# Rows of the first head pair placed by selection matmuls, and the first four pairs processed by halves of their queries

## The chip, the cores and the metric

The kernel runs on one core of one Trainium2 chip. The metric is the device time of one execution in microseconds. Five engines take part, each with its own instruction queue: PE (matmul; PEld is its weight load), DVE (VectorE), ACT (ScalarE), POOL (GpSimd) and SP (SyncE, which here only issues DMAs).

## The reference

Two layers over x of shape (4, 1024, 256): attention with 16 heads of 16 elements, and a mixture of 8 experts (top 2, capacity 1.25), each followed by a residual sum and a layer norm.

```
q, k, v = x @ wq.T, x @ wk.T, x @ wv.T                # per head, 16 elements
q_mag, k_mag = softplus(q), softplus(k)
q_embed = [q_mag * cos(freqs), q_mag * sin(freqs)]     # 32 elements per head
k_embed = [k_mag * cos(freqs + bias), k_mag * sin(freqs + bias)]
out = softmax(q_embed @ k_embed.T / 4) @ v             # all 1024 keys, no mask
x = layernorm(x + out @ wo.T)
gates = softmax(x @ router_w + router_b); top 2, positions by cumsum, capacity 640
y = sum of gate * (gelu(x @ w1 + b1) @ w2 + b2) over the chosen experts
x = layernorm(x + y)
```

## The kernel before

One program in three parts: a head that loads and prepares, a loop of attention steps, and the experts. The change touches the head and the attention loop; the experts stay as they are.

**Tiling of attention.** A batch has 1024 tokens and 16 heads. Heads go in two groups of eight (index f), each group in four pairs; a pair of one batch is a *unit* u, 32 units in all (`B * NU`). Of a unit, `qk_u` holds four tiles of 128 rows by 1024 columns: for each of the two heads the queries and the keys, as float32r values split in an upper part and a remainder, so that one product over 128 rows gives a score at full precision (for q the rows are cos/sin of the upper part twice, then of the remainder twice; for k the upper part, the remainder, and both again).

**Embedding.** `embedding(b, f, w, h)` makes q or k of all eight heads of a group for one half h of the tokens: a product (L367), softplus by ACT as Abs, Exp, Ln (L384 to L386), then sums, the product with the cos/sin table (L396) and the split in parts (L401 to L405). With `fast` the elementwise work is on DVE and ACT, otherwise on POOL. Its rows come out ordered by element and then head (d, m). The parts are stored in DRAM by four DMAs (L413), and `load_qk(u)` (L419) loads those of one pair, ordered as `qk_u` needs them: 8 DMAs for q (L432) and 4 for k (L436). DRAM is thus what puts rows in another order. In the head, unit 0's rows are stored and loaded by halves of the tokens, k through SP's queue, q through POOL's.

**A step.** Steps run over n = 0 to 255; step n handles unit n // 8 and a block c of 128 keys. It makes `key_scores` (L715: keys by queries, all 1024 queries of both heads, four products of 512 columns), subtracts the row maximum by a product of two rows with ones (`exponentials`, L730), lets ACT take exp (L737, two of 128x1024), and weights the values of the *step before* with them (`weighted_values`, L751). The maximum must be known before a unit's first step: `score_half(u, k, j)` (L688, queries by keys, 512 keys) with a DVE maximum each (L692), 32 of them per unit, then `max_parts` (three small DVE instructions, L698 to L700) and `max_rows` (four transposes on PE, L706, and a copy by ACT, L708). Unit 0's 32 scores stand in the head; from step 1 on each step carries four scores for the unit after (step 0 carries eight more). The results of a unit are copied by ACT (L760) and sent to DRAM and to another tile by six DMAs (`collect`, L779, L782).

**What sets the order.** All of this is under `manual_schedule`: each engine takes its instructions in the order in which the program text emits them. Pieces of other work (embeddings of the next group or batch, transposes, projections, the router) hang in a table `todo`, put there by `at` and `staged` at fixed places (batch, pair, block), and are emitted at the end of that step. Generators (`yield`) cut a piece in parts that are emitted at different places.

**Buffers.** PSUM: three banks `bank` (scores, embeddings, transposes), two double banks `st` (key scores; in the head `rotate` hands them out to others too), one `av`. SBUF pools: `big` (three: weights in duplicate, table 0, then `qk`), `p2` tag `parts`, `p4` tag `pt` (exponentials).

Lines of the profile that matter here: L367 embedding product, L413 store of parts, L432/L436 loads of `qk`, L688/L692 score and maximum, L698 to L708 the maxima's way to a row, L715/L730/L737/L751 a step, L238 store of a table.

## Time and profile before

| what | us |
|---|---|
| median of 3 runs (lowest, highest) | 1468.1 (1467.44, 1471.71) |
| the profiled execution, its own time | 1469.84 |
| its span, first to last instruction | 1468.0 |
| PE busy in the span | 1372.4 (93%) |
| DVE busy | 917.8 (63%) |
| ACT busy | 728.6 (50%) |
| POOL busy | 410.2 (28%) |
| start of the first exponential (step 0) | 64.06 |
| start of the exponentials of step 8 and step 32 | 102.23 and 188.76 |

A matmul's end is modelled, so a busy PE is not PE at its peak: what a piece of work costs is read better from how far apart two like steps start. In the rows of instructions the columns are start, length, engine, line, operation, output<-input, count, and in brackets the idle time before and what ended it.

### The profile page before, as it was taken

The page shows a single profiled execution, that of the slowest core. Times are in us where ns is not written, and L with a number is a line of the kernel's source. Part 1 is how long each engine was busy: PE and PEld are TensorE (multiplying, and loading weights), DVE is VectorE, ACT ScalarE, POOL GpSimd, SP SyncE. Part 2 cuts the span into 40 slices and gives each one's busy share as a digit, 9 for nine tenths or more (in the row PEclk, how much of TensorE's full clock was granted, in tenths as well). Part 3 has the DMA queues.
Part 4 walks back from the last instruction along what each step waited for, and adds up shares of the span by engine and source line. Part 5 has one row for each costly group of instructions (what it writes and reads, how often), then busy time and mean ns, then how long its engine had stood idle before and what let it go on. Part 6 is the DMA issues. An engine that isn't in the chain of part 4 may idle for free. (4 is left out here: it accounts for less than half of the span.)

```text
span 1468.0 us, 24361 instructions
## 1 busy us (share of the span) xinstructions
PE 1372.4 (93%) x9314; PEld 860.1 (59%) x9314; DVE 917.8 (63%) x1990; ACT 728.6 (50%) x944; POOL 410.2 (28%) x436
## 2 busy tenths in 40 slices
PE   5899999999999999999999999999994599999996
PEld 3455556555655565656556555555543377777775
DVE  6767766667877766787766677787715243333334
ACT  5365666565556656555664754655462222222221
POOL 5640043340002646000064520000402224434432
PEclk8799999999999999999999999999996699999998
DMA  7856367374344646453474542243210454333211
GB/s 234 262 161 186 99 189 201 89 226 119 108 120 137 190 128 212 122 153 88 116 216 134 151 135 63 71 105 84 76 58 7 131 181 154 107 115 130 72 40 43
DMA packets 107315, 191.23 MB, mean 130 GB/s; under 512 B 19633, under 2 KB 56178, under 8 KB 107072
## 3 DMA queue, kind: packets, MB, share of 16 engines
q1 hardware_dynamic: 96192, 167.80, 39.6%
q0 software_dynamic: 9888, 20.01, 4.4%
q10 hardware_dynamic: 1120, 1.87, 0.4%
q8 instruction: 73, 1.20, 0.4%
q14 instruction: 42, 0.34, 0.1%
HBM read 119.32 MB, written 73.63 MB: 131 GB/s over the span
## 5 line engine op out<-in xcount | busy, mean ns | idle before, releaser
L692 DVE TENSOR_REDUCE nm<-s 128x1 f32<-128x512 f32 x1024 | 644.6, 683 | 231.7 <-PE s L688 217.3
L737 ACT ACTIVATE pt<-st 128x1024 f32<-128x1024 f32 x512 | 496.2, 1021 | 392.7 <-PE st L730 375.8
L688 PE MATMUL s<-qk 128*128 128x512 f32 x1024 | 390.7, 440 | 23.7 <-DVE nm L692 12.1
L715 PE MATMUL st<-qk 128*128 128x512 f32 x1024 | 308.9, 401 | 4.4 <-ACT pt L737 3.4
L751 PE MATMUL av<-pt,va 128*32 128x256 f32 x4096 | 275.6, 386 | 0.5 <-ACT pt L737 0.5
L688 PEld LDWEIGHTS s<-qk 128*128 128x128 f32 x1024 | 179.9, 191 | 136.6 <-DVE nm L692 58.2
L715 PEld LDWEIGHTS st<-qk 128*128 128x128 f32 x1024 | 182.8, 189 | 68.1 <-ACT pt L737 33.2
L751 PEld LDWEIGHTS av<-pt,va 128*32 128x32 f32 x4096 | 107.2, 109 | 108.2 <-issue 63.0
L652 POOL DMA_INDIRECT slots_in<-held,scatter_idx x64 | 62.6, 977 | 306.0 <-DVE scatter_idx L650 225.1
L390 POOL TENSOR_TENSOR soft_q<-y_q,soft_q 128x512 f32<-128x512 f32 x14 | 17.9, 1279 | 448.0 <-ACT soft_q L386 448.0
L1234 PE MATMUL op<-w,h 128*128 128x256 f32 x640 | 140.6, 379 | 0.0
L1215 PE MATMUL hp<-slots_t,w 128*128 128x320 f32 x512 | 139.8, 434 | 0.0
L1234 PEld LDWEIGHTS op<-w,h 128*128 128x128 f32 x640 | 121.1, 190 | 17.0
L730 PE MATMUL st<-mt,ones_r 2*128 2x512 f32 x1024 | 130.1, 498 | 0.7 <-ACT mt L708 0.7
L1215 PEld LDWEIGHTS hp<-slots_t,w 128*128 128x128 f32 x512 | 97.7, 191 | 39.9 <-ACT slots_t L1068 0.3
L730 PEld LDWEIGHTS st<-mt,ones_r 2*128 2x128 f32 x1024 | 49.2, 182 | 90.0 <-issue 88.6
L1222 ACT ACTIVATE h<-hp,b_sb 128x640 f32<-128x640 f32 x64 | 50.8, 793 | 85.3 <-PE hp L1215 73.0
L1249 DVE TENSOR_TENSOR o<-op,b_sb 128x256 f32<-128x256 f32 x35 | 14.8, 424 | 103.7 <-PE op L1234 99.8
L1250 ACT ACTIVATE o<-o,w 128x256 f32<-128x256 f32 x35 | 17.8, 507 | 109.1 <-DVE o L1249 100.3
L1252 POOL DMA_INDIRECT y_rank<-o,rows x35 | 35.6, 1016 | 109.3 <-ACT o L1250 61.5
L1176 POOL DMA_INDIRECT out_dram<-row,rows x40 | 41.3, 1033 | 44.8 <-DMA out_dram<-row,rows 14.3
L463 DVE TENSOR_TENSOR held<-po,held 128x512 f32<-128x512 f32 x32 | 22.1, 690 | 41.8 <-PE po L455 41.8
(210 smaller groups left out, 1038.3 us busy)
## 6 DMA issues: line engine op xcount, KB each, us to landing
qk<-embed_q SPq DMA_DIRECT2D x248, 128.0 KB
qk<-embed_k SPq DMA_DIRECT2D x124, 256.0 KB
embed_k<-parts_k SPq DMA_DIRECT2D x64, 256.0 KB
w<-in_w_dram SPq DMA_DIRECT2D x16, 1024.0 KB
embed_q<-parts_q SPq DMA_DIRECT2D x56, 256.0 KB
y_rank<-zero SPq DMA_DIRECT2D x8, 1024.0 KB
tab_k<-table SPq DMA_DIRECT2D x14, 512.0 KB
tab_q<-table SPq DMA_DIRECT2D x12, 512.0 KB
```

Of the source, the lines that this page charges most:

```text
L652: nc.gpsimd.indirect_dma_start(out=scatter_views[2 * t + k], out_offset=bass.IndirectOffsetOnAxis(ap=scatter_idx[:, k, t : t + 1], axis=0) ...
L688: nc.tensor.matmul(ps, qk[:, 2 * h, lo : lo + P], qk[:, 2 * h + 1, j * HS : (j + 1) * HS], start=True, stop=True,)
L692: nc.vector.tensor_reduce(nms[u][:, j, i, s : s + 1], ps, AX.X, ALU.max, negate=True)
L715: nc.tensor.matmul(ps[:, f, :], qk[:, 2 * h + 1, c * P : (c + 1) * P], qk[:, 2 * h, f * HS : (f + 1) * HS], start=True, stop=False,)
L730: nc.tensor.matmul(tiles[h][:, f, :], ones_r[rows, :], mts[u][rows, :], start=False, stop=True,)
L737: nc.scalar.activation(pt, tiles[h], AF.Exp)
L751: nc.tensor.matmul(av[32 * s : 32 * (s + 1), cols], va[f][:, c, 2 * p + h, :], pt[h][:, s // 2, cols], start=(c == 0 and n == 0), stop=(c ...
L1176: nc.gpsimd.indirect_dma_start(out=out_views[t], out_offset=bass.IndirectOffsetOnAxis(ap=to[:, 0, t : t + 1], axis=0), in_=row[:, t, :], i ...
L1215: nc.tensor.matmul(ps[:, i, 0:half], w1_sb[:, k, c * P : (c + 1) * P], s_t[:, k, i * half : (i + 1) * half], start=(k == 0), stop=(k == KC ...
L1222: nc.scalar.activation(h_t[:, c, :].rearrange("p (i n) -> p i n", i=2), ps[:, :, 0:half], AF.Gelu, bias=b1_sb[:, e, c : c + 1],)
L1234: nc.tensor.matmul(ps, h_t[:, c, t * P : (t + 1) * P], w2_sb[:, c, :], start=(c == 0), stop=(c == HC - 1),)
L1252: nc.gpsimd.indirect_dma_start(out=y_views[e * ST + t], out_offset=bass.IndirectOffsetOnAxis(ap=to[:, 1, t : t + 1], axis=0), in_=o_sb, in ...
```

## The change

1. **Selection matrices.** POOL builds `picks`, float32r matrices of zeros and ones (two memsets, four selects, two copies), in the head, after its loads of angles.
2. **Unit 0's rows by matmul.** `move_first(w, cols, parts)` multiplies the four parts of an embedding by these matrices: for each of the two heads four products of 512 columns accumulate in one PSUM bank and give the tile in the order that `qk_0` needs; ACT copies it. There are four calls (k and q, two halves of the tokens): 32 products and 8 copies. No load from DRAM for unit 0 remains. The stores of the parts remain (the other pairs load them), now all on SP.
3. **Second half of q on POOL.** `embedding(0, 0, "q", 1)` is no longer `fast`.
4. **Half units.** The first four pairs (batch 0, group 0) are split in two by their queries: 36 entries in `units`, a half unit has 4 steps, and each step handles two blocks of keys for 512 queries. The number of steps stays 256, with the same products in each. A half unit has its own 16 scores, `max_parts`, `max_rows`, copy of results and `collect`.
5. **A plan of scores.** A list `ahead[n]` replaces the fixed four per step: the scores of all units from 1 on are spread so that each is done two steps before its unit starts, and no unit's before the pair ahead of it is about to start. It gives 6 in step 0, 5 in steps 1 to 18, and 4 from step 19 on. Ahead of step 0 stand the 16 scores of half unit 0 only, in place of 32.
6. **Other pieces of the head.** q of group 1 (batch 0) moves from the head into the steps, beside k (starting in steps 2, 5, 8, 11). The second key table is written in pieces: its first half before `max_parts(0)`, its second in steps 1 and 3. The stores of the tables and the load of the second pair come behind the last part of q.

```diff
+        picks = p1.tile([P, 2, 2, 13, HD], F32R, tag="os", name="picks")
+        for h in range(2):
+            pick = p2.tile([P, 2, 13, HD], F32, tag="y", name=f"pick_{h}")
+            nc.gpsimd.memset(pick, 0.0)
+            for w, (first, apart) in enumerate(((5, 2), (3, 4))):
+                blocks = pick[:, w, first : first + apart + 1 : apart, :]
+                nc.gpsimd.affine_select(
+                    out=blocks, in_=blocks, compare_op=ALU.not_equal, fill=1.0, base=-h,
+                    pattern=[[0, 2], [-FH, HD]], channel_multiplier=1,
+                )
+            nc.gpsimd.tensor_copy(picks[:, h], pick)
...
             for i, c in enumerate((nb4, sb4)):
                 nc.scalar.activation(a[:, i, :], cs[:, 1 - i, cols], AF.Copy, scale=c[:, 1:2])
                 nc.scalar.activation(kt[:, i, :], cs[:, i, cols], AF.Copy, scale=cb4[:, 1:2])
-            for i in range(2):
                 nc.gpsimd.tensor_tensor(kt[:, i, :], kt[:, i, :], a[:, i, :], ALU.add)
+                if i == 0:
+                    yield
             store_table(2, h, kt)
...
+        def move_first(w, cols, parts):
+            if 0 not in qks:
+                qks[0] = big.tile([P, 4, S], F32R, tag="big", name="qk_0")
+            k = w == "k"
+            pss = [bank(f"rows_{w}_{h}_{cols.start}", True) for h in range(2)]
+            for p in range(2):
+                for c in range(2):
+                    at = c + (2 if k else 4) * p
+                    first = (3 if k else 5) - at
+                    for h in range(2):
+                        nc.tensor.matmul(
+                            pss[h],
+                            picks[:, h, int(k), first : first + 8, :].rearrange("p b d -> p (b d)"),
+                            parts[p][:, c, :],
+                            start=(p == 0 and c == 0),
+                            stop=(p == 1 and c == 1),
+                        )
+                yield
+            for h in range(2):
+                nc.scalar.copy(qks[0][:, 2 * h + k, cols], pss[h])
+                yield
...
+        for i in range(B * NU):
+            for h in range(2) if i < NU // NF else (None,):
+                starts.append(starts[-1] + lasting[-1] if units else 0)
+                units.append((i, *divmod(i // (NU // NF), NF), i % (NU // NF), h))
+                lasting.append(NT if h is None else NT // 2)
...
+            for x in range(2):
+                h, q, k = (t, x, c) if half is None else (x, half, 2 * c + t)
                 nc.tensor.matmul(
-                    ps[:, f, :],
-                    qk[:, 2 * h + 1, c * P : (c + 1) * P],
-                    qk[:, 2 * h, f * HS : (f + 1) * HS],
+                    ps[:, x, :],
+                    qk[:, 2 * h + 1, k * P : (k + 1) * P],
+                    qk[:, 2 * h, q * HS : (q + 1) * HS],
...
-                if b == 0 and n > 1:
-                    staged(0, ((0, 2), (0, 4))[n - 2], 2, embedding, 0, 1, w, h)
+                if b == 0:
+                    staged(0, ((0, 2), (0, 5), (1, 0), (1, 3))[n], 2, embedding, 0, 1, w, h)
...
+            n_items = max([-((given - i) // (d - n + 1)) for d, i in due if d >= n], default=0)
+            most = max(i for first, i in may if first <= n)
+            ahead[n] = items[given : min(given + n_items, most)]
...
             k0, q0, k1, q1 = first("k", 0), first("q", 0), first("k", 1), first("q", 1)
...
-            load_qk(0, halves[0], "k")
-            for work in (k1, q0, q0):
+            mk0, mq0 = moving("k", 0), moving("q", 0)
+            for work in (mk0, mq0, mk0, mq0):
                 run(work)
-            load_qk(0, halves[0], "q", nc.gpsimd)
             key_table(1)
-            for work in (k1, q1, q1, k1, k1):
+            for work in (k1, q1, mk0, mq0, k0, q0):
                 run(work)
-            load_qk(0, halves[1], "k")
-            for work in (q1, q1):
+            run(k1)
+            mk1 = moving("k", 1)
+            for work in (mk0, mq0):
                 run(work)
-            load_qk(0, halves[1], "q", nc.gpsimd)
             for h in range(2):
                 values(0, 0, h, rotate=True)
-            load_qk(1)
+            for i in range(4):
+                score_half(0, 2 * i, 0)
+            for work in (mk1, mk1, mk1, mk1, k1, q1):
+                run(work)
+            mq1 = moving("q", 1)
+            for i in range(4):
+                score_half(0, 2 * i + 1, 0)
+            for h in range(2):
+                values(0, 1, h, rotate=True)
+            for i in range(4):
+                score_half(0, 2 * i, 1)
+            for i in range(4):
+                score_half(0, 2 * i + 1, 1)
+            for _ in second_key_table(0):
+                pass
+            max_parts(0)
+            max_rows(0, rotate=True)
+            for work in (mq1, mq1, mq1, mq1, q1):
+                run(work)
             for h in range(2):
                 store_table(0, h, cs[:, :, halves[h]])
                 store_table(1, h, kt0[:, :, halves[h]])
+            once("k", 1)
+            once("q", 1)
+            load_qk(1)
             late_constants()
...
+        pieces = second_key_table(1)
+        for c in (1, 3):
+            at(0, 0, c, run, pieces)
```

The lines of the changed kernel that the text names: L452 the selection products, L786 key scores.

## The prediction

> **What bounds the kernel now.** I read the 40 slices first, then busy time by stretches of 3.4 us in the head, then the timeline of ACT, which gives one pair of exponentials per step, then what PE waits for.
>
> ```profile
> PE   5899999999999999999999999999994599999996
> PEclk8799999999999999999999999999996699999998
> ```
>
> From the third slice on PE is full, so what is moved there costs its PE time, and what can be won lies in the first two slices (36.7 us each). There it looks like this (columns: stretch, its length, then busy us and instructions of PE, PEld, DVE, ACT, POOL, then the granted clock, DMA share, GB/s):
>
> ```profile
> 21.40:24.80 3.40, 2.03 (x19) 1.84 (x17) 3.40 (x7) 3.27 (x6) 1.87 (x4) 1.00 0.80 295
> 24.80:28.20 3.40, 0.00 (x0) 0.00 (x0) 3.33 (x6) 1.41 (x3) 1.68 (x4) 1.00 0.70 237
> 28.20:31.60 3.40, 0.01 (x1) 0.04 (x1) 3.40 (x9) 3.20 (x6) 3.40 (x7) 0.50 0.86 263
> 55.50:58.90 3.40, 2.00 (x4) 0.74 (x4) 3.40 (x7) 0.43 (x1) 2.82 (x3) 1.00 0.21 55
> 65.80:69.20 3.40, 3.40 (x7) 1.85 (x7) 3.40 (x7) 0.20 (x1) 0.00 (x0) 0.50 0.89 219
> 69.20:72.60 3.40, 3.40 (x11) 1.97 (x10) 2.43 (x5) 0.00 (x0) 0.00 (x0) 0.50 1.01 245
> ```
>
> PE has nothing from 23.4 to 31.6 (rows on their way to DRAM and back) and then runs scores at the pace of DVE's maxima, one per 0.60 us. The clock is 0.50 from 28.2 to 38.4 and from 58.9 to 72.6. PE's waits in the head are these:
>
> ```profile
> PE s L688 <- DVE parts_q L405: 8.2, 1, 8.2
> PE mp L706 <- DVE m L700: 3.1, 1, 3.1
> PE s L688 <- DMA qk<-embed_q: 2.2, 1, 2.2
> ```
>
> The steps, from ACT's timeline (start, us):
>
> ```profile
> 64.06 1.94 ACT L737 ACTIVATE pt<-st 128x1024 f32<-128x1024 f32 x2 [1.28 <-PE st L730]
> 73.87 1.94 ACT L737 ACTIVATE pt<-st 128x1024 f32<-128x1024 f32 x2 [7.88 <-PE av L751]
> 78.37 1.94 ACT L737 ACTIVATE pt<-st 128x1024 f32<-128x1024 f32 x2 [2.56 <-PE av L751]
> 102.23 1.94 ACT L737 ACTIVATE pt<-st 128x1024 f32<-128x1024 f32 x2 [1.45 <-PE st L730]
> 123.23 1.94 ACT L737 ACTIVATE pt<-st 128x1024 f32<-128x1024 f32 x2 [1.56 <-PE st L730]
> 126.73 1.94 ACT L737 ACTIVATE pt<-st 128x1024 f32<-128x1024 f32 x2 [1.56 <-PE st L730]
> 130.59 1.94 ACT L737 ACTIVATE pt<-st 128x1024 f32<-128x1024 f32 x2 [1.43 <-PE st L730]
> 188.76 1.94 ACT L737 ACTIVATE pt<-st 128x1024 f32<-128x1024 f32 x2 [1.44 <-PE st L730]
> ```
>
> Step 0 is at 64.06, step 8 at 102.23, step 32 at 188.76. A plain step takes 3.50 us (123.23 to 126.73); one that has a unit's max_rows takes 3.86 (126.73 to 130.59), so max_rows costs 0.36. Steps with an embedding's two products go from 86.03 to 91.41, 5.38: the products cost 1.88. Steps with a transpose_x take 3.87 (165.94 to 169.81), 0.37.
>
> From step 32 on (pair 4) the changed kernel does the same in the same order with the same scores made ahead, 4 per step. So the forecast is one number: the time of step 32, against 188.76.
>
> **When step 0 comes.** I follow the new order engine by engine, each instruction after the one ahead of it and after what it waits for, with durations from the trace. Up to 21.2 nothing differs (the last cast of parts_q, 19.96 to 21.18). The picks, on POOL behind the last load of angles (12.1), are seven small instructions like its neighbours (0.2 to 0.6 us each): ready by 16, used at 19.9, cost nothing.
>
> (1) The first four L452 products run at 19.9 to 21. The next for q's second head has the PSUM slot of ep_q_1 and waits until ACT has read it: ACT does Abs, Exp, Ln of k's second half (21.1 to 23.0), then Relu and Abs of q's second half, to 24.2. Everything on PE is queued behind it. Eleven products at 0.27 (two scores in a row take 0.54) end at 27.2.
> (2) ACT copies the first two tiles (0.58 each) after its Ln (25.6), to 27.2, casts parts_k_1 (1.22) to 28.4, copies the other two to 29.6. DVE subtracts (1.29) to 29.2. PE meanwhile makes values(0,0): 32 products took 3.73, to 30.7.
> (3) Four scores; k's second-half products wait for banks that DVE frees one per 0.60, from 32.3 to 34.5; four more scores to 35.7; values(0,1), 3.73, to 39.5; eight scores of the second key half at DVE's pace, 0.54 + 7 x 0.60 + 0.69, to 44.9; max_parts 1.5 (the row at 95.17 to 96.63, POOL busy beside it), to 46.4.
> (4) Transposes 1.1 at the low clock (61.04), eight L452 products for q's second half at 0.43, to 51; their parts have been ready since 33, made by POOL (1.27 + 2.5 + 1.17 + 2.5 from 25.6), so that way is hidden; it decides only if POOL is over 14 us late. Copy 0.6, two scores, four L786, two scores, two L800: step 0 at 55.2.
>
> Half clock, from 24.8 or so, would add some 2 us. Here a rule and the trace differ. The Trainium skill, "TensorE: Matmul & The Clock Gate", Part 1, says that the clock falls after an idle window of about 3.4 us; PE's gap here is 3.2 (21.0 to 24.2), so by the rule alone it stays up and step 0 is at 55.2, or 53 if it also stays up through (3). But the trace lost the clock at 58.9, after a window in which PE was busy 2.00 of 3.40, and did not get it back in one with 3.40 of 3.40 at DVE's pace. So thin work is enough. I take the fall in (3) for sure, the one at 24.8 for half: **step 0 at 56.0**, with 53 and 58 as ends; 8 us ahead of 64.06.
>
> **What lies between step 0 and step 32.** In before: 188.76 - 64.06 = 124.7, of which the first two steps took 14.3 at the low clock. In after:
> - 32 steps at 3.50: 112.0. Step 0 has no av product yet, and steps 0 to 3 followed singly take 13.9, as the sum of their parts with 0.4 left over.
> - 8 max_rows in place of 4 (four units are eight halves): 8 x 0.36 = 2.9.
> - 16 scores that were made ahead of step 0 and now come in steps: 5 per step in steps 1 to 18, 6 in step 0. 16 x 0.27 = 4.3.
> - four embeddings' products for the second f, where before two stood ahead of step 0: 4 x 1.88 = 7.5; four transpose_x, 1.5.
> That is 128.2 + 0.4.
> - Banks. Scores have three, and each is free when its maximum is done. With four scores DVE needs 2.48 of 3.50 us; with five, 3.1 of 3.77. A plain five-score step just fits (the fourth score needs the bank of the first, free 1.6 after it, and comes at 1.74). Not where max_parts comes between: it stands behind the fifth maximum and takes 0.62 (123.60 to 124.22) or 1.46 with POOL at work,
>
> ```profile
> 123.60 0.17 DVE L698 TENSOR_TENSOR nm<-nm 128x16 f32<-128x16 f32 x1
> 95.17 0.34 DVE L698 TENSOR_TENSOR nm<-nm 128x16 f32<-128x16 f32 x1
> 95.54 0.53 DVE L699 CAST m<-nm 128x16 fp32r<-128x16 f32 x1
> ```
>
> and the next step's fourth score then waits 0.6 or 1.4. This falls on steps 6, 10 (POOL at work) and 14, 18 (not): 4.1; step 2's is covered by the embedding behind it. max_rows takes a bank too, 0.3 x 5. Together 5.6; no row shows it, so the ends are 0 and 12 (0.4 in every five-score step and 1.4 at each of the five). I take 5.6, nearest to the rows.
>
> Step 32: 56.0 + 128.6 + 5.6 = 190.2, **1.4 us later than 188.76**.
>
> **What is moved on the queues.** Before, POOL carried q's stores and loads of the first pair (24 issues) and SP k's. After, no load of the first pair is left; 16 stores stay, all on SP, with nobody waiting but the second pair's load. SP's store of table 2 waits for POOL's addition, behind ACT's four scalings behind values(0,1): 44.1. Behind it stand q's last stores, four table stores, 12 loads of the second pair: 21 issues at 0.6 to 0.9 and 5.5 MB at 300 GB/s (303 to 338 in 58.9 to 65.8) from 44.1 end at 62.5, landed by 65. PE asks for the first of it in step 3, at about 67: hidden by 2 us, and cost is 1 us per us if that cover is gone. The third pair's load waits for ACT's last scaling (step 3), lands near 80, asked for in step 10, past 90. In steps 4 to 31 twice as many collects (12 DMAs per pair) queue on SP with slack of steps.
>
> **The sum.** The profiled execution took 1469.84 with a span of 1468.0; 1.84 lies around the span. 1468.0 + 1.4 + 1.84 = 1471.2 on its own time, 1.7 above the median of the runs (1468.1) like the profiled one: **1469.5**. A measurement of this kernel can tell about 0.3%, 4.4 us, from no change: the forecast is no change that can be told.
>
> **Rivals.**
> A, faster: DVE keeps up (the three max_parts rows at 0.17 to 0.19, most steps with slack at the banks) and the clock stays up in the head. Banks 1 in place of 5.6, step 0 at 53 or 54: 182.6 to 184, about 1462. For it: a plain five-score step fits; against: POOL is busy in steps 4 to 15.
> B, slower, the other side: the second pair's rows land late. Everything in SP's queue after 44 hangs on the one store that waits for POOL. With the addition at 48 and 250 GB/s (245 at 69.2) the last row lands at 48 + 22 + 2.5 = 72.5, 4 to 5 us after PE asks, and an idle PE loses its clock for 3.4 us or more, half of it lost: 1476. It decides from an addition later than about 46.
> C, slower: DVE is the bound of the five-score steps. Banks cost 12: 1476.
> D, the change does not do it: ACT, which empties every moved tile, and the waits of (1) to (3) eat the gain, step 0 stays near 62 to 64: 1476 to 1477.
>
> **How the numbers follow.** Forecast 0.40; A 0.27; B 0.10; C 0.15; D 0.08. The likeliest's own range is 1464 to 1473, from the ends of step 0 and part of the banks'. A reaches to 1460, B to D to 1478: 1460 to 1478 holds 8 in 10. Faster by over 0.3% is A, 0.27; same 0.40; slower 0.33.
>
> **What would show it.** Right: step 0 near 56 with steps 0 to 1 and 1 to 2 under 4.3 us; PE waiting for the maxima after steps 6, 10, 14 and 18; no wait of a score for DMA in step 3; step 32 near 190. Wrong: step 0 below 53 or above 59, plain five-score steps at another time than 3.77, a PE wait on qk<-embed, or a difference between step 32 and the end that is not the same as before (1279.2 us).

## The result and the profile after

| | before | after |
|---|---|---|
| median of 22 runs each (lowest, highest), us | 1468.33 (1464.69, 1471.71) | 1473.97 (1467.18, 1478.14) |
| the profiled execution, its own time | 1469.84 | 1476.15 |
| its span | 1468.0 | 1474.3 |
| start of step 0 | 64.06 | 53.25 |
| start of step 32 | 188.76 | 194.83 |
| step 32 to the end of the span | 1279.2 | 1279.5 |

The ratio is 1.0035, 95% interval 1.0024 to 1.0045: slower by some 5 us. The head gave 10.8 us, and the 32 steps behind it took 141.6 us in place of 124.7. What comes after step 32 is unchanged, so all of the loss lies between step 0 and step 32.

The 40 slices of the changed kernel, PE's busy tenths and its clock:

```profile
PE   7899999999999999999999999999995499999997
PEclk9999999999999999999999999999997699999999
```

The first two slices went from 5 and 8 tenths to 7 and 8, and their clock from 8 and 7 to 9 and 9: the head is fuller. The loss is too small to be seen in a slice. ACT's timeline has it (changed kernel; start, length; the pair of exponentials of steps 0, 1, 10, 11, 12, 14, 15, 16 and 32):

```profile
53.25 1.94 ACT L807 ACTIVATE pt<-st 128x1024 f32<-128x1024 f32 x2 [2.15 <-PE st L800]
56.94 1.94 ACT L807 ACTIVATE pt<-st 128x1024 f32<-128x1024 f32 x2 [1.75 <-issue]
...
98.85 1.94 ACT L807 ACTIVATE pt<-st 128x1024 f32<-128x1024 f32 x2 [1.71 <-PE st L800]
104.96 1.94 ACT L807 ACTIVATE pt<-st 128x1024 f32<-128x1024 f32 x2 [4.16 <-PE st L800]
112.57 1.92 ACT L807 ACTIVATE pt<-st 128x1024 f32<-128x1024 f32 x2
...
120.13 1.94 ACT L807 ACTIVATE pt<-st 128x1024 f32<-128x1024 f32 x2 [1.98 <-PE st L800]
126.78 1.94 ACT L807 ACTIVATE pt<-st 128x1024 f32<-128x1024 f32 x2 [4.70 <-PE st L800]
133.69 1.94 ACT L807 ACTIVATE pt<-st 128x1024 f32<-128x1024 f32 x2 [2.94 <-PE st L800]
...
194.83 1.94 ACT L807 ACTIVATE pt<-st 128x1024 f32<-128x1024 f32 x2 [1.45 <-PE st L800]
```

Steps 0 to 1 take 3.69. But 10 to 12 take 13.72 and 14 to 16 take 13.56. A plain five-score step has 3.6 to 3.9 in this trace; steps 11 and 15 also carry other work, so that the fair measure is what the same steps take in a run without the hold-up (reduce_parts below: 10.39 and 8.86). In both places ACT sits idle for over 4 us, waiting for PE. What PE waited for between 18 and 200 us (waits of the changed kernel: total, times, longest):

```profile
PE s L746 <- DVE nm L750: 4.6, 4, 2.2
PE rows_q L452 <- ACT soft_q L400: 3.0, 1, 3.0
PE mp L774 <- DVE m L768: 1.9, 1, 1.9
PE s L746 <- DMA wo_sb<-in_wo_dram: 0.6, 1, 0.6
```

The waits of 8.2 and 2.2 us for parts and rows in the head are gone; the second and third line are what the new head waits for. New behind step 0 is the first line: scores wait for a PSUM bank that a maximum has not yet freed, twice for about 2 us. What DVE did before the two long ones (timeline of DVE, changed kernel):

```profile
100.89 0.93 DVE L766 TENSOR_TENSOR nm<-nm 128x8 f32<-128x8 f32 x1
101.86 1.20 DVE L767 CAST m<-nm 128x16 fp32r<-128x16 f32 x1
103.09 0.19 DVE L768 TENSOR_TENSOR m<-nm,m 128x16 f32<-128x16 f32 x1
...
122.11 1.20 DVE L766 TENSOR_TENSOR nm<-nm 128x8 f32<-128x8 f32 x1
123.34 1.20 DVE L767 CAST m<-nm 128x16 fp32r<-128x16 f32 x1
124.58 0.19 DVE L768 TENSOR_TENSOR m<-nm,m 128x16 f32<-128x16 f32 x1
```

What POOL did meanwhile (its timeline; x2 stands for two operations in a row):

```profile
99.26 2.54 POOL L427 TENSOR_TENSOR parts_q<-e_q,parts_q 128x512 fp32r<-128x512 f32 x2
101.75 1.27 POOL L406 TENSOR_TENSOR soft_k<-y_k,soft_k 128x512 f32<-128x512 f32 x1
...
121.99 2.51 POOL L427 TENSOR_TENSOR parts_k<-e_k,parts_k 128x512 fp32r<-128x512 f32 x2
```

And the score that stood behind them (timeline of PE, the wait in brackets):

```profile
103.93 0.50 PE L746 MATMUL s<-qk 128*128 128x512 f32 x1 [1.93 <-DVE nm L750]
```

These are the three small instructions of `max_parts`. They handle 8 or 16 values per partition and take 0.16 to 0.19 us each when POOL is idle, as in step 6, just ahead of the start of POOL's block at 83.28 (timeline of DVE, changed kernel):

```profile
82.84 0.16 DVE L766 TENSOR_TENSOR nm<-nm 128x8 f32<-128x8 f32 x1
```

In steps 10 and 14 two of the three take 0.93 to 1.20: each ends about when a large elementwise operation of POOL (1.27 us) ends. The fifth maximum of step 10 was done at 100.9; the next maximum starts only after `max_parts`, at 103.2, and PE's fourth score of step 11 waits 1.93 us for it. Then the clock goes (changed kernel by stretches; PE, PEld, DVE, ACT, POOL busy us, then the granted clock, DMA share, GB/s):

```profile
101.80:105.20 3.40, 1.47 (x14) 0.67 (x17) 3.33 (x7) 0.24 (x1) 1.22 (x1) 1.00 1.04 241
105.20:108.60 3.40, 3.40 (x21) 1.84 (x12) 1.16 (x2) 2.28 (x3) 0.00 (x0) 0.51 0.55 129
...
122.30:125.70 3.40, 1.20 (x5) 0.62 (x4) 3.33 (x5) 0.00 (x0) 2.20 (x2) 1.00 0.84 248
125.70:129.10 3.40, 3.40 (x23) 1.32 (x23) 1.45 (x3) 1.94 (x2) 0.00 (x0) 0.51 1.09 367
129.10:132.50 3.40, 3.40 (x12) 2.89 (x11) 1.98 (x3) 0.59 (x1) 0.00 (x0) 0.50 1.08 390
```

In the stretches that hold the waits PE is busy for 1.47 and 1.20 of 3.40 us; in those behind them it is busy throughout, but at half clock, for 3.4 us after the first wait and 6.8 after the second.

### The profile page after: what moved, and what is told of

The parts are those of the page before. It is cut to its first block, busy times and chain, and to the rows that moved or that the text cites. A ratio compares the mean times of both kernels' runs of the same rounds, so it can differ in the third digit from the quotient of the medians.

```text
span 1474.3 us, 24497 instructions
## 1 busy us (share of the span) xinstructions
PE 1384.6 (94%) x9362; PEld 870.2 (59%) x9362; DVE 925.1 (63%) x1997; ACT 735.0 (50%) x959; POOL 411.0 (28%) x427
## 3 DMA queue, kind: packets, MB, share of 16 engines
q8 instruction: 74, 1.21, 0.4%
## 5 line engine op out<-in xcount | busy, mean ns | idle before, releaser
L786 PE MATMUL st<-qk 128*128 128x512 f32 x1024 | 307.4, 401 | 2.9 <-ACT pt L807 2.9
L786 PEld LDWEIGHTS st<-qk 128*128 128x128 f32 x1024 | 185.0, 190 | 64.2 <-ACT pt L807 28.4
L1355 POOL DMA_INDIRECT y_rank<-o,rows x35 | 35.7, 1019 | 112.7 <-ACT o L1353 61.2
L412 POOL TENSOR_TENSOR e_k<-soft_k,tab_k 128x512 f32<-128x512 f32 x28 | 35.5, 1290 | 49.0 <-DMA tab_k<-table 48.6
```

Source lines behind the costliest of these rows:

```text
L786: nc.tensor.matmul(ps[:, x, :], qk[:, 2 * h + 1, k * P : (k + 1) * P], qk[:, 2 * h, q * HS : (q + 1) * HS], start=True, stop=False,)
L1355: nc.gpsimd.indirect_dma_start(out=y_views[e * ST + t], out_offset=bass.IndirectOffsetOnAxis(ap=to[:, 1, t : t + 1], axis=0), in_=o_sb, in ...
```

## The experiments

The theory was: `max_parts`, held up by POOL, in steps 10 and 14, and the clock that each hold-up costs, are the loss. Rivals: DVE's throughput as such is the bound of five-score steps; the second pair's rows are late; the half units or the selection products cost by themselves. The runs were made in three groups on different chips, each beside the kernel before (medians 1465.46, 1469.53 and 1470.44 us), so ratios to it are compared, not times; the first row of the table is the result above. Step 0 and step 32 are those of each profiled execution.

| run | ratio to before (95%) | step 0 | step 32 | between |
|---|---|---|---|---|
| changed kernel | 1.0035 (1.0024, 1.0045) | 53.25 | 194.83 | 141.6 |
| after_again | 1.0036 (1.0024, 1.0047) | 54.50 | 194.16 | 139.7 |
| late_scores | 1.0013 (1.0003, 1.0022) | 53.88 | 190.27 | 136.4 |
| pool_parts | 1.0078 (1.0064, 1.0091) | 53.29 | 202.22 | 148.9 |
| reduce_parts | 0.9987 (0.9978, 0.9996) | 56.71 | 189.77 | 133.1 |
| load_first | 0.9994 (0.9982, 1.0006) | 54.99 | 194.44 | 139.5 |
| full_units | 1.0092 (1.0077, 1.0107) | 74.22 | 200.61 | 126.4 |
| full_units2 | 1.0024 (1.0003, 1.0046) | 64.37 | 192.50 | 128.1 |
| three | 0.9987 (0.9974, 0.9999) | 53.99 | 189.09 | 135.1 |
| before_reduce | 0.9977 (0.9968, 0.9987) | 62.64 | 186.22 | 123.6 |
| best | 0.9977 (0.9964, 0.9991) | 51.53 | 185.32 | 133.8 |
| best_swap | 0.9962 (0.9945, 0.9978) | 51.97 | 187.30 | 135.3 |

**The changed kernel again.** No edit.

> The changed kernel once more, unedited, beside the kernel before on the chip on which the edits run, so that they can be set against it. If the POOL block that holds up max_parts is started by a transfer (the rows of a table from DRAM), the steps in which the two meet differ from run to run: the waits for maxima stand in other steps than 11 and 15, or are of other sizes, and the times of single runs spread over more than 6 us, as they did (1467 to 1478), with a ratio to the kernel before of 1.002 to 1.005.

The ratio repeats (1.0036). The expectation that the waits would stand in other steps or have other sizes was hardly met: the hold-up stands in the same two steps, with waits of 2.03 and 2.25 us in place of 1.93 and 2.20. But in step 14 it now takes other instructions (timeline of DVE, the changed kernel's second profiled execution):

```profile
122.89 0.21 DVE L766 TENSOR_TENSOR nm<-nm 128x8 f32<-128x8 f32 x1
123.14 1.23 DVE L767 CAST m<-nm 128x16 fp32r<-128x16 f32 x1
124.40 1.19 DVE L768 TENSOR_TENSOR m<-nm,m 128x16 f32<-128x16 f32 x1
```

PE's waits behind it, in steps 11 and 15 (its timeline):

```profile
104.64 0.51 PE L746 MATMUL s<-qk 128*128 128x512 f32 x1 [2.03 <-DVE nm L750]
126.24 0.49 PE L746 MATMUL s<-qk 128*128 128x512 f32 x1 [2.25 <-DVE nm L750]
```

So which of the three is held is a matter of a few tenths of a microsecond between two engines that do not wait for each other. The single runs spread over 13 us (1468.0 to 1480.7), as do those of the kernel before beside them (1465.4 to 1479.2, 51 runs), so the spread shows nothing of the cause. No wait of a score for a transfer shows in step 3 here.

**The fourth and fifth score behind the weighted values.**

```diff
+                if n + 1 in starts and n < 32:
+                    fourth, rest = [], fourth + rest
                 for f, *args in first:
```

> One edit in the changed kernel: in the steps that follow a max_parts (steps 3, 7, 11 and so on, up to 31) the fourth and fifth score are emitted behind the step's eight weighted-values products, where before the fourth stood between the key scores and the subtraction of the maxima. Same work, other order. Theory (the 6 us lost up to step 32 come from the fourth score's wait for a bank behind a max_parts that POOL holds up, and from the clock that this wait costs): the scores' waits for maxima in steps 11 and 15 fall from 1.9 and 2.2 us to under 0.6, the stretches at half clock from 105.3 and 125.7 go, step 32 comes at 187 to 190, and the time is 5 to 8 us below the changed kernel's. Rival (DVE as such is the bound of five-score steps, in whatever order): step 32 within 1.5 us of 194.8 and the time within 2 us of the changed kernel's.

`max_parts` is still held (0.82 and 1.22 us at 101.6), but PE has eight weighted-values products to do meanwhile. The score's wait falls to 0.40, and the clock stays (stretches of late_scores, columns as above):

```profile
103.20:106.60 3.40, 2.80 (x23) 1.34 (x24) 3.37 (x7) 2.06 (x3) 0.47 (x1) 1.00 0.98 236
106.60:110.00 3.40, 3.40 (x12) 1.96 (x11) 1.61 (x3) 1.97 (x4) 0.00 (x0) 1.00 0.48 125
```

Steps 10 to 12 take 11.27 (13.72), 14 to 16 take 9.77 (13.56). Step 32 comes at 190.27, just outside the expected 187 to 190, and the ratio is 3.2 us (0.0022) below the changed kernel's, less than the 5 to 8 expected. The same work in another order wins this much, so DVE's throughput is not the bound. The order has its own price in the four-score steps, though: 22 to 24 and 30 to 32 take 7.80 (7.35 and 7.36 in the changed kernel).

**The two small instructions on POOL.**

```diff
...
+                nc.vector.tensor_reduce(
+                    low, nm[:, :, :, 0:2].rearrange("p j i s -> p i s j"), AX.X, ALU.min
+                )
...
+                nc.gpsimd.tensor_copy(upper.bitcast(F32R), whole)
+                nc.gpsimd.tensor_tensor(lower, whole, upper, ALU.subtract)
```

> One edit in the changed kernel: for half units 1 to 7 the minimum over the two key halves is a reduction with one input on DVE (in place of a sum-like operation with two), and the two small instructions behind it (cast and difference) go to POOL. The order of everything else stays. Theory (the small DVE instructions wait for POOL's large ones): DVE's part of max_parts falls from 2.4 us in steps 10 and 14 to 0.2 to 0.4, the wait of the fourth score behind it to under 0.6 us, the half clock after it goes, and step 32 comes at 187 to 190, 5 to 8 us earlier. If the reduction also waits for POOL, some 1.2 us stay of 2.4 and the gain is 2 to 5 us. Rival (the maxima themselves fill DVE): no more than 1.5 us. A second risk is that the two instructions on POOL stand behind an embedding's and max_rows waits for them: then PE shows a wait of mp for POOL.

A miss, and the risk named last was what happened. DVE is free of the hold-up (its reduction takes 0.16 to 0.17 us all seven times, also at 117.6, beside a product of POOL that ran from 116.4 to 119.0), but POOL takes its work in order. Its queue stood for 18.3 us behind a product that waited for a table's rows from DRAM, and both small instructions behind it (timeline of POOL, pool_parts):

```profile
86.06 2.52 POOL L412 TENSOR_TENSOR e_q<-soft_q,tab_q 128x512 f32<-128x512 f32 x2 [18.32 <-DMA tab_q<-table]
```

`max_rows` then waited for POOL (PE's waits, pool_parts):

```profile
PE mp L783 <- POOL m L777: 12.9, 1, 12.9
```

This also shows what sets the time at which POOL's block starts here: the arrival of the table.

**One-input reductions on DVE.** All of `max_parts` stays on DVE and in its place; only the form of the instructions changes, for half units 1 to 7.

```diff
-            nc.vector.tensor_tensor(low, low, high, ALU.min)
-            nc.vector.tensor_copy(upper.bitcast(F32R), whole)
-            nc.vector.tensor_tensor(lower, whole, upper, ALU.subtract)
+            if units[w][4] is None or w == 0:
...
+            else:
+                two = small.tile([P, 2, 4, 2, 2], F32, tag="two", name=f"two_{w}")
+                least = nm[:, :, :, 0:2].rearrange("p j i s -> p i s j")
+                for t in range(2):
+                    nc.vector.tensor_reduce(upper[:, :, t].bitcast(F32R), least, AX.X, ALU.min)
+                nc.vector.tensor_reduce(two[:, 0, :, :, 0], least, AX.X, ALU.min)
+                nc.vector.tensor_reduce(
+                    two[:, 0, :, :, 1], upper[:, :, 0].unsqueeze(3), AX.X, ALU.max, negate=True
+                )
+                for t in range(2):
+                    nc.vector.tensor_reduce(lower[:, :, t], two[:, 0], AX.X, ALU.add)
```

> One edit in the changed kernel: max_parts of half units 1 to 7 is six reductions on DVE with one input each (minimum straight into the upper part, the lower part as a sum over a pair of minimum and negated upper part), in place of a two-input minimum, a cast and a two-input difference. Everything stays on DVE and in its place. Theory (the two-input operation and the cast are held while POOL runs a large elementwise operation, a reduction with one input is not): six times 0.17 us, 1.0 us, in every step, also where POOL is at work, in place of 0.53 us alone and 2.4 to 3.7 us beside POOL; scores wait for maxima at most 1 us in a step, no half clock behind it, time 3 to 6 us below the changed kernel's. Rival (any small DVE operation is held by POOL): six reductions beside POOL take 3 us or more, and the time is the changed kernel's or worse.

This decides it. In step 10 POOL runs just as before, and DVE passes beside it. POOL's timeline in reduce_parts:

```profile
102.39 2.54 POOL L427 TENSOR_TENSOR parts_q<-e_q,parts_q 128x512 fp32r<-128x512 f32 x2
```

DVE's:

```profile
103.73 0.25 DVE L774 TENSOR_REDUCE m<-nm 128x8 fp32r<-128x16 f32 x2
103.88 0.17 DVE L775 TENSOR_REDUCE two<-nm 128x8 f32<-128x16 f32 x1
103.96 0.16 DVE L776 TENSOR_REDUCE two<-m 128x8 f32<-128x8 f32 x1
104.16 0.25 DVE L780 TENSOR_REDUCE m<-two 128x8 f32<-128x16 f32 x2
```

PE's, with the one wait of that step:

```profile
105.05 0.50 PE L746 MATMUL s<-qk 128*128 128x512 f32 x1 [0.23 <-DVE nm L750]
```

And the stretch around it (columns as above):

```profile
101.70:106.00 4.30, 4.07 (x33) 2.10 (x34) 3.51 (x12) 1.93 (x2) 4.30 (x5) 1.00 1.03 242
```

Six reductions, from 103.73 to the next maximum at 104.32, take 0.6 us, with POOL busy all the while. In step 14 (121.61 to 122.29) POOL is at work too, and none is held. PE waits 0.23 in place of 1.93, and the clock stays at 1.00. Steps 10 to 12 take 10.39, 14 to 16 take 8.86: 8.0 us of the 8.5 that lie between step 0 and step 32. The ratio falls from 1.0036 to 0.9987, by 7.2 us, a little over the expected 3 to 6. Nothing was taken from DVE but the time for which it was held.

**The second pair's load ahead of the tables.**

```diff
+            for work in (mq1, mq1, mq1, mq1, q1):
+                run(work)
+            load_qk(1)
             for _ in second_key_table(0):
                 pass
             max_parts(0)
             max_rows(0, rotate=True)
-            for work in (mq1, mq1, mq1, mq1, q1):
-                run(work)
...
-            load_qk(1)
```

> One move in the changed kernel: the eight products and two copies that move q's second half, its last stores and the load of the second pair stand ahead of the second key table and of max_parts(0), in place of behind them. Theory: the load no longer waits for POOL's addition, so step 3's wait of 0.6 us for rows goes, and the eight products fill PE's wait of 1.9 us for the maxima, so step 0 comes 1 to 2 us earlier; but the waits of steps 11 and 15 for maxima stay as they are, and with them most of the loss: step 32 at 192 to 194, time 1 to 3 us below the changed kernel's. Rival (the second pair's late rows and the thin head are what costs): 5 us or more below.

PE's wait for `m` and the wait for rows are gone, but a wait of 1.0 us for the row of maxima takes their place, and step 0 is not earlier. The waits in steps 11 and 15 did not stay, though I had expected it; the hold-up moved to step 6, where POOL's block now starts at the very moment (timeline of DVE, load_first):

```profile
83.72 1.26 DVE L766 TENSOR_TENSOR nm<-nm 128x8 f32<-128x8 f32 x1
85.01 1.20 DVE L767 CAST m<-nm 128x16 fp32r<-128x16 f32 x1
86.25 1.19 DVE L768 TENSOR_TENSOR m<-nm,m 128x16 f32<-128x16 f32 x1
```

POOL's:

```profile
83.67 2.51 POOL L412 TENSOR_TENSOR e_q<-soft_q,tab_q 128x512 f32<-128x512 f32 x2 [14.27 <-DMA tab_q<-table]
```

All three are held, 3.65 us, and PE waits 3.3. This profiled execution (1469.54) is the slowest of this kernel's 14 runs; the lowest is 1461.39. The median gains 6 us (ratio 0.9994), as the rival said. I can't say from it that late rows were the cause: in the trace step 32 is at 194.44, as late as in the changed kernel. A table that arrives at another time, so that in most runs the two engines do not meet, would give such a median, but the runs without a profile do not show it: open. What the record does show is that the gain does not come on top of that of the reductions: with both, the ratio is 0.9987 (three) and 0.9977 (`best`), against 0.9987 with the reductions alone, and the intervals overlap. So late rows are not a second loss of this size.

**Full units, selection products kept.** All 32 scores of unit 0 again ahead of step 0.

```diff
-            for h in range(2) if i < NU // NF else (None,):
+            for h in (None,):
...
+            for j in range(2):
+                for i in range(8):
+                    score_half(0, 4 * (i // 2) + 2 + i % 2, j)
             for _ in second_key_table(0):
                 pass
             max_parts(0)
...
```

> The changed kernel with full units: the selection products stay, the halving by queries goes. All 32 scores of unit 0 then stand ahead of step 0 (16 more at 0.60 us, 9.6 us), and steps carry 4 scores from step 4 on, 5 in steps 0 to 3. Also the last products that move q's rows and the load of the second pair stand ahead of the scores of the second query half and of the second key table, since the second pair is asked for in step 0. Theory (the selection products are worth what the head lost, and the five-score steps lost it again): step 0 at 62 to 64, step 32 some 122 to 125 later, at 184 to 188; time 1 to 5 us below the kernel before. Rival (half units are what gains, and the selection products alone only trade one wait for another): step 0 at 64 or later, step 32 at 189 or later, the time not below that of the kernel before.

The theory missed. The rival's numbers came (74.22, 200.61, no gain), but for a reason that neither had named: PE waited for the second pair's rows (waits of full_units):

```profile
PE s L746 <- DMA qk<-embed_k: 7.6, 2, 6.7
```

Their buffer is freed by two copies of weights on DVE, which stood behind all 32 maxima, so the load began at 61.2. With the copies moved ahead of values(0,1):

```diff
+            once("k", 1)
+            once("q", 1)
             for h in range(2):
                 values(0, 1, h, rotate=True)
...
-            once("k", 1)
-            once("q", 1)
```

> As full_units, with the two copies of weights that free the buffer of the second pair (on DVE) ahead of the products of values(0,1), so that its rows can be loaded from about 40 us on; in full_units the load waited for these copies until 61 us and step 0 came at 74. Theory: 32 scores at 0.60 us in the head again; the maxima end at 60 to 62, step 0 at 63 to 66, step 32 some 125 later at 188 to 191: the selection products without half units win nothing against the kernel before (64.06 and 188.76), ratio 0.999 to 1.003. Rival (the selection products are what takes 8 us from the head): step 0 at 60 or earlier, time 3 us or more below the kernel before.

Step 0 is at 64.37, against 64.06 before: the selection products alone take nothing from the head. It comes 9.4 us later than in load_first (54.99), which has half units and the same head but for the place of the two copies, and 10.4 and 12.8 later than in three and `best`, which have the copies there too. The 16 scores that half units leave out (16 x 0.60 = 9.6) are thus about the whole gain; the rest goes with the clock, which was 0.91 from 12 us to step 0 here, and 0.88, 0.92 and 0.96 in those three. Between step 0 and step 32 it takes 128.1, more than the 125 expected, so that step 32 (192.50) missed the expected 188 to 191: here too `max_parts` met POOL, in step 14 (0.51, 1.22 and 1.21 us), PE waited 1.3, and the stretch behind it has a clock of 0.68. So the hold-up is not bound to half units.

**Three edits at once** (late scores, reductions, the load ahead of the tables with its buffer freed early).

> The changed kernel with three edits at once: the fourth and fifth score of the step behind a max_parts emitted behind the weighted values (as in late_scores), max_parts of half units as one-input reductions (as in reduce_parts), and the second pair's load with the last of q's rows ahead of max_parts(0), its buffer freed by copies ahead of values(0,1). Theory: step 0 at 53 to 55, no wait for maxima over 0.6 us, no wait for rows in step 3, no half clock after step 0, step 32 at 186 to 189, time 0 to 3 us below the kernel before (ratio 0.998 to 1.000) and 5 to 8 us below the changed kernel. Rival (five scores in 3.8 us cost PE more than its own time whatever the order): step 32 at 190 or later, time at or above the kernel before.

Step 32 at 189.09, at the edge of the 186 to 189 of the theory, and a ratio of 0.9987, inside its range and no better than the reductions alone. Once `max_parts` is no longer held, the late order looks like a cost only: 135.1 between step 0 and step 32, against 133.1 in reduce_parts and 133.8 in `best`.

**The reductions in the kernel before.**

```diff
+            if u == 0:
...
+            else:
...
+                least = nm.rearrange("p j i s -> p i s j")
+                nc.vector.tensor_reduce(m[:, :, :, 0].bitcast(F32R), least, AX.X, ALU.min)
+                nc.vector.tensor_reduce(two[:, :, :, 0], least, AX.X, ALU.min)
+                nc.vector.tensor_reduce(
+                    two[:, :, :, 1], m[:, :, :, 0].unsqueeze(3), AX.X, ALU.max, negate=True
+                )
+                nc.vector.tensor_reduce(m[:, :, :, 1], two, AX.X, ALU.add)
```

> One edit in the kernel before: max_parts of units 1 to 31 is four reductions with one input on DVE, in place of a two-input minimum, a cast and a two-input difference; all else as before. In the trace of before these three took 343, 338 and 270 ns on average where they take 184, 190 and 174 alone, 12.8 us more in all over 32 units, but the steps carry four scores and have slack at the banks. Theory: little of this lies on the path, since with four scores the next fourth score's bank is free in time: ratio 0.998 to 1.000. Rival (what the reductions won in the changed kernel has nothing to do with half units, and they win as much in any): ratio 0.996 or less, as much as the 0.005 between the changed kernel with and without them.

0.9977: 3.4 us, more than expected and less than the rival's 0.996. The groups of instructions show that the reductions are not held: over 31 units the means of the four are 177 to 190 ns, where the three instructions that they replace had means of 270 to 343 in the kernel before. One of the four (before_reduce; behind the bar busy us and mean ns):

```profile
L705 DVE TENSOR_REDUCE m<-nm 128x16 fp32r<-128x32 f32 x31 | 5.9, 190 | 1.1
```

The traces place only part of the gain: 1.1 us between step 0 and step 32 and 1.2 from there to the last step. Step 0 itself, which the edit does not touch, came 1.4 earlier. The rest stays open.

**The versions that beat both.** `best` is the changed kernel with reductions in all units but the first and the load as in three; `best_swap` also lets ACT do q's second half ahead of k's:

```diff
-            for work in (k1, q1, mk0, mq0, k0, q0):
+            for work in (q1, k1, mk0, mq0, k0, q0):
```

> The changed kernel with one-input reductions in max_parts of all units but the first, and the second pair's load and the last of q's rows ahead of max_parts(0) (the buffer freed ahead of values(0,1)); scores stay in their order. Against three it leaves the late scores out, which in steps 19, 23, 27 and 31 made two steps take 7.8 us in place of 7.4. Theory: step 0 at 54 to 55, 133 us from step 0 to step 32 as in reduce_parts, step 32 at 187 to 188, time 3 to 5 us below the kernel before (ratio 0.9965 to 0.998). Rival (the load ahead of the tables only makes other transfers late): step 32 at 189 or later, ratio as in reduce_parts, 0.9987.

> As best, with one swap in the head: ACT does the Relu, Abs, Exp and Ln of q's second half ahead of those of k's second half. PE's wait of 3.0 us for ACT's Abs of q (the first of the moved rows' products standing behind it) should fall to about 1.1, the copies of the first rows come 0.8 us earlier, k's rows of the second half up to 2.6 us later, which the four scores and the values cover. Theory: the half clock from 23.3 on goes, step 0 0.8 to 2 us earlier than in best. Rival (k's second half is then late): PE waits for k's parts ahead of its second half's products, step 0 not earlier.

`best` has step 0 at 51.53, earlier than the expected 54 to 55, 133.8 between, as the theory said, and a ratio of 0.9977, inside the range that the theory gave. The swap did to PE's wait what was said of it (3.0 to 1.1 us), and gave it back at once: PE then waits 1.7 us for k's second half (values' products behind DVE's sum) and 1.0 for ACT's copy of the values. The half clock from 23.3 did go, as the theory said, but two other stretches ran at half clock, from about 43.6 and 53.9. Its step 0 is at 51.97, not earlier; the rival was right on that. This profiled execution (1472.98) is the slowest of its nine. Its ratio, 0.9962, is the lowest, but its interval overlaps that of `best`.

## Why the prediction was right or wrong

The time lies within the range, and above the forecast of 1469.5 and the likeliest's own range of 1464 to 1473. Step 32 was forecast 1.4 us late and came 6.1 and 5.4 us late in the two profiled executions. The likeliest case was no change that can be told, with 4.4 us as the measure; the 5 us measured are slower by that measure, a case that had 0.33. That the total is not further off is in part luck, since two errors pull against each other: in the profiled execution step 0 came 2.7 us earlier than forecast, and what lies behind it took 7.4 us more. By its steps:

**Step 0: right in kind, and within its ends.** Forecast 56.0, ends 53 and 58; 53.25 and 54.50, and in the three edited kernels whose head is the same 53.29, 53.88 and 56.71. The block of PE behind ACT was there (3.0 us, forecast 3.2). The half clock came twice, from 23.3 and from 47.2, for 3.4 us each:

```profile
19.90:23.30 3.40, 0.53 (x2) 0.19 (x1) 3.40 (x7) 3.34 (x6) 0.00 (x0) 1.00 0.80 308
23.30:26.70 3.40, 3.28 (x8) 2.60 (x9) 3.37 (x5) 1.74 (x4) 1.75 (x2) 0.51 0.60 227
...
43.80:47.20 3.40, 1.37 (x7) 0.88 (x7) 3.15 (x11) 0.00 (x0) 3.07 (x9) 1.00 0.36 141
47.20:50.60 3.40, 3.22 (x8) 2.00 (x6) 0.00 (x0) 1.16 (x3) 0.00 (x0) 0.50 1.06 407
```

So the trace was the better guide than the rule on idle windows: a gap of 3.0 us was enough, in a stretch in which PE was still busy for 0.53 of 3.40 us. "For sure" in (3) held, but it cost less than taken. Much of the scatter of step 0 goes with this: from 12 us to step 0 the clock was 0.92 in the changed kernel (53.25), 0.88 in its second profiled execution (54.50) and 0.85 in reduce_parts (56.71).

**Between step 0 and step 32: the sum of the parts came near, the term for banks failed.** 128.6 was worked out without banks. reduce_parts, where no instruction is held, took 133.1. PE's waits there add up to 1.2 us; the other 3.3 stand in no term, and what they are is open. Plain five-score steps took 3.64 (12 to 13) to 3.92 (13 to 14), 3.77 forecast. One count was off without harm: the plan has 20 scores above four per step (2 in step 0, 18 behind it), not 16; the four, 1.1 us, are about what step 0 saves by having no weighted values yet (1.07 us in a later step). But the banks' term was 5.6, with 12 as its upper end, and what lies above 128.6 measured 13.0 and 11.1 (141.6 and 139.7); of this, 8.5 and 6.6 are above reduce_parts. Beside the row that the term took its 1.46 from (95.17 to 96.63 in the kernel before), POOL ran casts (timeline of POOL, before):

```profile
95.42 1.17 POOL L403 CAST parts_k<-e_k 128x512 fp32r<-128x512 f32 x2
```

The term failed in three ways:
- *size*: I took `max_parts` beside POOL at 1.46, from this row (casts of 0.59 us each, and the small instructions took 0.34 to 0.53). Beside POOL's two-input operations (1.27) it took 2.32 and 2.59. Each of the three can be held for as long as POOL's operation lasts;
- *place*: POOL was put at steps 6 and 10. It waited 15.6 us for the table's rows, began at 83.28, just as `max_parts` of step 6 ended, and was at work in 10 and 14;
- *what follows*: the term had the wait alone. Of the 8.0 us that reductions took out of steps 10 to 12 and 14 to 16, the waits are 3.6 (4.1 less the 0.5 that stay); the other 4.4 are, by subtraction, the clock that PE lost behind them (10.2 us at half clock would make 5.1). I had weighed the clock only for the head.

The Trainium skill, "SBUF — State Buffer", section "Who interferes with whom", speaks of this, and I had not brought it to bear: DVE and POOL share one pair of ports, and whoever starts first holds it for the whole instruction. A DVE operation with two SBUF inputs contends with a POOL operation that reads SBUF, a cast can contend, and `tensor_reduce` on this chip never does. The traces agree: up to 1.26 us beside POOL's two-input operations, where reductions took 0.16 to 0.17. That the port is what holds them is the page's explanation; the runs show that the instruction's form decides.

**The second pair's rows: cover thinner than forecast.** The store of the table was issued at 45.1 (forecast 44.1), and a score waited 0.6 us in step 3 of one profiled execution and not in the other. (The profile puts the wait down to `wo_sb`, the transfer queued right behind these rows; with the load moved ahead, in load_first, it is gone.) The 2 us of cover were used up, not more.

**First steps and remainder: right.** 3.69 and 3.84 for steps 0 to 1 and 1 to 2 (under 4.3), 1279.5 behind step 32 (1279.2).

**The rivals.** C gave the nearest time (1476; banks 12), by a mechanism that is not the one found: DVE's pace in every five-score step. late_scores and reduce_parts gain with the same number of scores, so C's cause falls and its number stands. A needed short `max_parts` rows; with the reductions, which make them so, the ratio is 0.9987, and A's 1462 would be 0.996. B decided nothing in the changed kernel's own trace, where it is 0.6 us; why load_first gained 6 us in the median is open. D did not happen.

**What the change is worth.** With reductions in both, the kernels stand at 0.9977 (`best`, which also has the earlier load; 0.9987 in reduce_parts, without it) and 0.9977 (before_reduce), so these runs tell no gain by the change: some 11 us less head (51.5 and 62.6), some 10 us more in the 32 steps (133.8 and 123.6).

## What to carry to other kernels

Work that is moved from an idle head into full steps keeps its price, and takes away slack that was hiding something else: look for the small instruction that stands in the queue of the engine that frees a buffer, and ask what its worst row in the trace is, beside which neighbour. When its length varies sevenfold between rows that do the same, change its form before its place: here six one-input reductions in place of three instructions won more than the late scores; against the earlier load the intervals overlap. And add to each new wait on PE the half clock that may follow it.

## What the runs showed of the hardware

- Beside a two-input operation of POOL a DVE minimum, cast or difference on 8 or 16 values per partition took up to 1.26 us, beside a cast of POOL 0.52 to 0.54, alone 0.16 to 0.19. It is held again for each instruction: three in a row took 3.65 us in load_first.
- One-input reductions on DVE took 0.16 to 0.17 us each beside the same POOL operations, and six followed each other within 0.6 us.
- Stretches of 3.40 us in which PE was busy for 0.53, 1.20, 1.37 and 1.47 us were followed by half clock for 3.4 or 6.8 us (changed kernel); one in which it was busy for 2.80 was not (late_scores). None of these stretches was idle throughout.
- Single runs spread over 11 and 13 us in the changed kernel and over 7 in reduce_parts (1463.6 to 1470.5), but over 14 in the kernel before beside them. That the chance meeting of the two engines makes the spread is not shown.
